# Score maxima taken over 32 tokens of four heads instead of 128 tokens of one, and a later place for the router's second choice, places and scatters

## The chip, the cores and the metric

The kernel runs on one core of one Trainium2 chip. The metric is the device time of one execution in microseconds; the median of several executions is compared. Before the change it is 818.26 us (three runs, 817.12 to 818.61).

## The reference

A transformer layer with attention and a mixture of experts, on x of 8 batches, 256 tokens and 256 features, in 32-bit floats. Cut to what matters here:

```python
q = rope(norm(x) @ Wq)              # 32 query heads of 8
k = rope(norm(x) @ Wk)              # 8 key heads of 8, each for 4 query heads
scores = einsum('bkgtd,bksd->bkgts', q, k) / sqrt(8)
scores = where(causal, scores, -inf)
attn = softmax(scores, axis=-1)
x = x + norm(einsum('bkgts,bksd->bkgtd', attn, v) @ Wo + b_out)

scores = sigmoid(norm(x) @ w_router.T)         # 8 routed experts
topk_w, topk_i = top_k(scores, 2)              # weights divided by their sum
out = sum over the two chosen experts of weight * ((silu(x@wg) * (x@wu)) @ wd)
out = out + two shared experts of the same form
x = x + norm(out)
```

A softmax subtracts each row's maximum before the exponential. A row here is one token of one query head, and its maximum runs over the keys up to that token.

## The kernel before

Tokens lie 128 to a tile, two tiles (tt or t = 0, 1) to a batch. The work up to the router is written as steps put on a timeline by the function `at(when, step, ...)`; the unit of `when` is one batch, and the steps are emitted in the order of `when`. Every engine then executes its own instructions in that order, so the timeline is an order and not a clock. After it come the routed experts, in blocks of 256 rows gathered by expert, and the final norm.

A batch goes through these steps. `project` (L342) multiplies by the weights and VectorE does the rotation of queries and keys (L362, L366, reading PSUM). `split` rounds queries and keys to a high and a low part on POOL. `keysT` and `queriesT` (L404, L436) transpose them on TensorE; the results go to `kst`, which holds the keys, and to `qA`, which holds the queries. In both, three key heads share the 128 partitions, in blocks of 32 rows (J = 3, and NS = 3 such groups c). In `kst` each key head has columns of its own and zeros outside its 32 rows, so one stationary tile of queries, 96 rows high, meets up to three key heads in one stream of columns.

Maxima: for a token tile, `maxima` (L461) computes the scores in PSUM. The stationary operand is one query head slot (group c, head g) of 128 tokens (L472); the columns are the keys of up to three key heads, 128 of them for the first token tile and 256 for the second. A second matmul (L479) adds the causal mask to the last 128 columns of each head, with an identity of 128 rows as the stationary operand. VectorE's reduce (L486) takes the maxima out of a PSUM bank of up to 512 columns. The generator `maxima_of` (L450) lists the calls: per batch 32 pairs of matmuls and 26 reduces. `split_shift` and `shiftT` (L494, L501) round the negated maxima to two parts, transpose them, and send them by three DMAs to rows 96 and up of `qA` (L516).

Weights: `weights_of` (L521) multiplies keys by queries with the shift among the rows (L524), ScalarE takes the exponential (L532) and POOL zeroes what the mask forbids (L534). `values` (L545) multiplies by the values with stationary operands of 32 columns, four side by side (L552). `softmaxed` (L564) transposes the result (L572) and divides.

PSUM: scores, weights and experts' products share five banks (`ps_mm`); transposes, projections, router logits and places share two (`ps_tp`), in turn, and the values' sums have one.

Router: `logits` (L661), then on VectorE `first_choice` (L688) and `second_choice` (L697). `places` (L717) has four small matmuls on TensorE that read the choice (L724, L727) and VectorE work that reads their result; `shares` (L710) makes the weights, and `scatter` (L743) multiplies on POOL and writes records to memory by indirect DMAs on POOL's queue. For all batches but the last, in units of a batch after a base a = b + 1.24, these stand at 0.27, 0.302, 0.37, 0.375 and 0.39. The second token tile's projection of batch b + 3 stands at a + 0.31.

The shared experts (`shared_gate_up`, `shared_down`, L780 and L793) are spread over the attention of later batches from b + 1.5 on.

Of the kernel before, what the change touches and what calls it, by code (L numbers as in the profile page):

```python
# [24 lines left out]
SHIFT = 96  # L25
# [5 lines left out]
def attn_moe_kernel(  # L31
# [47 lines left out]
    nc = tc.nc  # L79
    B, T, D = x.shape  # L80
# [11 lines left out]
    G = 4  # L92
    NKV = NH // G
    NK = NKV * HD
    NC = NKV // G
    J = 3
    NS = -(-NKV // J)
    KR = SHIFT + 2 * J
    QSCALE = HD**-0.5
    FT = 4  # L100
    NTOK = NT * P
# [45 lines left out]
    for b in range(1, B):  # L147
# [6 lines left out]
    nc.scalar.dma_start(out=wr_sb, in_=wr)  # L154


    mask = aconst.tile([P, P], BF16, name="mask")
    nc.gpsimd.memset(mask, 0.0)
    nc.gpsimd.affine_select(
        out=mask,  # L160
        in_=mask,
        pattern=[[-1, P]],
        compare_op=ALU.is_ge,
        fill=NEG,
        base=0,
        channel_multiplier=1,
    )
    ident_b = aconst.tile([P, P], BF16, name="ident_b")
    nc.vector.tensor_copy(ident_b, ident)
    ident_r = aconst.tile([P, P], F32R, name="ident_r")  # L170
    nc.vector.tensor_copy(ident_r, ident)

# [14 lines left out]
    qAs, ksts, v_aug = {}, {}, {}  # L187

    def clear_operands(i):
        qAs[i] = aconst.tile([P, NS * G, T], F32R, name=f"qA_{i}")  # L190
        engine = nc.gpsimd if i > 0 else nc.vector
        engine.memset(qAs[i][:, (NS - 1) * G :, :].bitcast(F32), 0.0)
# [106 lines left out]
    def at(when, step, *args):  # L299
        timeline.append((when, len(timeline), step, args))  # L300
# [100 lines left out]
    def heads_in(c):  # L401
        return min(J, NKV - c * J)
# [33 lines left out]
    def queriesT(b, tt, c):  # L436
        qs = held["qs", b, tt][1]
        n = heads_in(c) * HB
        pt = ps_tp.tile([P, G, P], F32, tag="tp", name=f"pqT{b}_{tt}_{c}")
        for g in range(G):  # L440
            nc.tensor.matmul(
                pt[0:n, g, :],
                lhsT=qs[:, c * G + g, 0:n],
                rhs=ident_r,
                start=True,
                stop=True,
            )
        nc.scalar.copy(qAs[b % 3][0:n, ts(c, G), ts(tt, P)], pt[0:n])

    def maxima_of(b, tt):  # L450

        width = (tt + 1) * P
        for c in range(NS):
            per = min(512 // width, heads_in(c))
            for k0 in range(0, heads_in(c), per):
                nk = min(per, heads_in(c) - k0)
                ng = 512 // (nk * width)
                for g0 in range(0, G, ng):
                    yield c, c * J + k0, nk, g0, ng

    def maxima(b, tt, c, k0, nk, g0, ng):  # L461

        qA, kst = qAs[b % 3], ksts[b % 3]
        if ("nmx", b, tt) not in held:
            held["nmx", b, tt] = small.tile(
                [P, NKV, G], F32, tag="nmx", name=f"nmx{b}_{tt}", bufs=2
            )
        nmx = held["nmx", b, tt]
        width = (tt + 1) * P
        sc = ps_mm.tile([P, ng, nk, width], F32, tag="mm", name="sc")  # L470
        for g in range(ng):
            nc.tensor.matmul(  # L472
                sc[:, g, :, :],
                lhsT=qA[0:SHIFT, c * G + g0 + g, ts(tt, P)],
                rhs=kst[0:SHIFT, k0 : k0 + nk, 0:width],
                start=True,
                stop=False,
            )
            nc.tensor.matmul(  # L479
                sc[:, g, :, width - P :],  # L480
                lhsT=ident_b,
                rhs=mask.unsqueeze(1).to_broadcast([P, nk, P]),
                start=False,
                stop=True,
            )
        nc.vector.tensor_reduce(  # L486
            nmx[:, k0 : k0 + nk, g0 : g0 + ng].rearrange("p k g -> p g k"),
            sc,
            AX.X,
            ALU.max,  # L490
            negate=True,
        )

    def split_shift(b, tt):  # L494
        nmx = held.pop(("nmx", b, tt))
        nhl = small.tile([P, NKV, 2, G], F32R, tag="nhl", name=f"nhl{b}_{tt}", bufs=2)
        nc.vector.tensor_copy(nhl[:, :, 1, :], nmx)
        nc.vector.tensor_tensor(nhl[:, :, 0, :], nmx, nhl[:, :, 1, :], ALU.subtract)
        held["nhl", b, tt] = nhl

    def shiftT(b, tt):  # L501
        nhl = held.pop(("nhl", b, tt))
        pm = ps_tp.tile([2 * NH, P], F32, tag="tp", name=f"pm{b}_{tt}")
        nc.tensor.matmul(
            pm,
            lhsT=nhl.rearrange("p k a g -> p (k a g)"),
            rhs=ident_r,
            start=True,
            stop=True,
        )  # L510
        nm = work.tile([2 * NH, P], F32R, tag="nm", name=f"nm{b}_{tt}")
        nc.vector.tensor_copy(nm, pm)
        for c in range(NS):
            n = 2 * heads_in(c)
            lo = c * J * 2 * G
            nc.sync.dma_start(  # L516
                out=qAs[b % 3][SHIFT : SHIFT + n, ts(c, G), ts(tt, P)].bitcast(F32),
                in_=nm[lo : lo + n * G, :].bitcast(F32),
            )

    def weights_of(b, kv, s, t):  # L521

        sc = ps_mm.tile([P, G, P], F32, tag="mm", name="scT")
        nc.tensor.matmul(  # L524
            sc,
            lhsT=ksts[b % 3][0:KR, kv, ts(s, P)],
            rhs=qAs[b % 3][0:KR, ts(kv // J, G), ts(t, P)],
            start=True,
            stop=True,
        )  # L530
        e = work.tile([P, G, P], F32, tag="ex", name="ex", bufs=EX)
        nc.scalar.activation(e, sc, AF.Exp, scale=QSCALE)  # L532
        if s == t:
            nc.gpsimd.affine_select(  # L534
                out=e,
                in_=e,
                pattern=[[0, G], [1, P]],
                compare_op=ALU.is_ge,
                fill=0.0,
                base=0,  # L540
                channel_multiplier=-1,
            )
        held["ex", b, kv, s, t] = e
# [535 lines left out]
    for b in range(B):  # L1079
# [15 lines left out]
        for tt in range(TT):  # L1095
            for m in maxima_of(b, tt):
                at(when, maxima, b, tt, *m)
                when += 0.032
            at(when + 0.001, split_shift, b, tt)
            at(when + 0.07, shiftT, b, tt)  # L1100
        last = b == B - 1
# [240 lines left out]
```

## Time and profile before

| | |
|---|---|
| median of the runs | 818.26 us |
| the profiled execution's own time | 817.86 us |
| its span, first to last instruction | 815.8 us |
| TensorE clock granted, mean | 0.970 |
| maxima's score matmuls, first and last start | 20.8 and 436.9 us |
| first routed expert's matmul | 548.6 us |

The profile follows one execution. PE is TensorE's matmuls, PEld its loads of stationary operands, DVE is VectorE, ACT ScalarE, POOL GpSimd and SP the engine that issues most DMAs. Busy time is a sum over an engine's instructions. Matmuls are pipelined: one is shown from its start to a modelled end, so that neighbours overlap and their durations add up to more than the time that they take.

In the slices each digit is the busy share of a fortieth of the span, in tenths. A group's row gives line, engine and operation; what is written and what is read; shapes as partitions by elements; the count; busy microseconds and the mean in nanoseconds; and, after the bar, the engine's idle time before these instructions with what ended most of it. A timeline's row gives the start in microseconds from the span's start, the time to the end of the last of the merged instructions, and their count. For matmuls the first shape is rows by columns of the stationary operand, the second the moving operand.

### The profile page before, as it was taken

The page shows a single profiled execution, that of the slowest core. Times are in us where ns is not written, and L with a number is a line of the kernel's source. Part 1 is how long each engine was busy: PE and PEld are TensorE (multiplying, and loading weights), DVE is VectorE, ACT ScalarE, POOL GpSimd, SP SyncE. Part 2 cuts the span into 40 slices and gives each one's busy share as a digit, 9 for nine tenths or more (in the row PEclk, how much of TensorE's full clock was granted, in tenths as well). Part 3 has the DMA queues.
Part 4 walks back from the last instruction along what each step waited for, and adds up shares of the span by engine and source line. Part 5 has one row for each costly group of instructions (what it writes and reads, how often), then busy time and mean ns, then how long its engine had stood idle before and what let it go on. Part 6 is the DMA issues. An engine that isn't in the chain of part 4 may idle for free. (4 is left out here: it accounts for less than half of the span.)

```text
span 815.8 us, 11856 instructions
## 1 busy us (share of the span) xinstructions
PE 761.7 (93%) x3977; PEld 579.3 (71%) x3977; DVE 492.2 (60%) x1412; ACT 251.3 (31%) x552; POOL 344.0 (42%) x620
## 2 busy tenths in 40 slices
PE   5989899999999999999999998799999999999992
PEld 3544467767776776776766657688888888888991
DVE  5756577667668568568666635547655555742226
ACT  2455344334334334333333431121111111111214
POOL 4567456426436436436324441416223434343323
PEclk8799899999999999999999998899999999999997
DMA  5033300000000000000000002365465665758544
GB/s 155 3 88 90 89 16 16 8 22 15 7 23 14 2 29 14 3 29 14 2 29 2 14 14 90 139 226 169 129 206 168 192 218 157 233 149 271 170 81 155
DMA packets 31011, 70.42 MB, mean 86 GB/s; under 512 B 8560, under 2 KB 25456, under 8 KB 28256
## 3 DMA queue, kind: packets, MB, share of 16 engines
q1 hardware_dynamic: 19504, 54.23, 19.2%
q0 software_dynamic: 8128, 9.77, 6.4%
q10 hardware_dynamic: 3312, 5.60, 2.4%
q8 instruction: 34, 0.56, 0.3%
q14 instruction: 33, 0.27, 0.1%
HBM read 55.16 MB, written 11.80 MB: 82 GB/s over the span
## 5 line engine op out<-in xcount | busy, mean ns | idle before, releaser
L780 PE MATMUL gu<-xgT,w 128*128 128x256 f32 (+1 forms) x840 | 163.9, 354 | 1.0 <-ACT xgT L978 0.7
L780 PEld LDWEIGHTS gu<-xgT,w 128*128 128x128 f32 x840 | 144.5, 190 | 18.1 <-ACT xgT L978 1.0
L532 ACT ACTIVATE ex<-scT 128x512 f32<-128x512 f32 x192 | 113.6, 597 | 137.4 <-PE scT L524 124.9
L780 PE MATMUL gu<-x2T,ws_sb 128*128 128x256 f32 x640 | 152.9, 385 | 0.1
L486 DVE TENSOR_REDUCE nmx<-sc 128x2 f32<-128x512 f32 (+2 forms) x208 | 129.3, 643 | 26.4 <-PE sc L479 26.1
L780 PEld LDWEIGHTS gu<-x2T,ws_sb 128*128 128x128 f32 x640 | 119.8, 193 | 21.3 <-ACT ex L532 3.8
L534 POOL TENSOR_SCALAR_AFFINE_SELECT ex<-ex 128x512 f32<-128x512 f32 x128 | 81.0, 639 | 114.3 <-ACT ex L532 114.1
L1014 POOL DMA_INDIRECT sums<-yb,of x37 | 58.5, 1582 | 109.2 <-DVE yb L1013 71.1
L472 PE MATMUL sc<-kst,qA 96*128 96x512 f32 (+2 forms) x256 | 101.3, 426 | 0.8 <-issue 0.5
L524 PE MATMUL scT<-qA,kst 102*128 102x512 f32 x192 | 97.5, 516 | 1.8 <-DMA qA<-nm 1.8
L1003 ACT ACTIVATE sg<-gu 128x256 f32<-128x256 f32 (+1 forms) x105 | 37.6, 358 | 191.1 <-PE gu L780 154.2
L991 DVE STREAM_TRANSPOSE xgT<-xg 32x128 f32<-32x128 f32 x240 | 72.6, 302 | 29.4 <-DMA xg<-rows,of 20.6
L793 PE MATMUL po<-w,act 128*128 128x256 f32 x370 | 83.1, 379 | 0.0
L793 PE MATMUL po<-ws_sb,sact 128*128 128x256 f32 x320 | 74.7, 391 | 4.6 <-DVE sact L816 4.6
L793 PEld LDWEIGHTS po<-w,act 128*128 128x128 f32 x370 | 69.8, 190 | 9.3
L793 PEld LDWEIGHTS po<-ws_sb,sact 128*128 128x128 f32 x320 | 61.6, 196 | 18.3 <-DVE sact L816 5.0
L479 PE MATMUL sc<-mask,ident_b 128*128 128x256 bf16 (+2 forms) x256 | 74.3, 293 | 0.0
L1004 DVE TENSOR_TENSOR act<-sg,gu 128x256 f32<-128x256 f32 (+1 forms) x105 | 38.8, 388 | 56.8 <-ACT sg L1003 56.2
L815 DVE SCALAR_TENSOR_TENSOR th<-th,gu 128x256 f32<-128x256 f32 x70 | 29.4, 419 | 65.8 <-ACT th L814 65.8
L932 POOL DMA_INDIRECT xg<-rows,of x37 | 35.9, 970 | 63.0 <-DMA of<-slots 47.4
L472 PEld LDWEIGHTS sc<-kst,qA 96*128 96x128 f32 x256 | 51.4, 201 | 13.6 <-issue 3.9
L552 PE MATMUL av<-ex,v_aug 128*32 128x512 f32 x384 | 58.3, 605 | 1.3 <-POOL ex L534 1.3
(171 smaller groups left out, 847.8 us busy)
## 6 DMA issues: line engine op xcount, KB each, us to landing
w<-in_routed SPq DMA_DIRECT2D x21, 1920.0 KB
ws_sb<-in_shared ACTq DMA_DIRECT2D x8, 480.0 KB
xs<-in_x SPq DMA_DIRECT2D x8, 256.0 KB
rows<-x2n SPq DMA_DIRECT2D x8, 256.0 KB
acc<-sums SPq DMA_DIRECT2D x4, 512.0 KB
sums<-ya SPq DMA_DIRECT2D x14, 128.0 KB
kst<-kA SPq DMA_DIRECT2D x16, 96.0 KB
out<-acc SPq DMA_DIRECT2D x6, 256.0 KB
```

Of the source, the lines that this page charges most:

```text
L472: nc.tensor.matmul(sc[:, g, :, :], lhsT=qA[0:SHIFT, c * G + g0 + g, ts(tt, P)], rhs=kst[0:SHIFT, k0 : k0 + nk, 0:width], start=True, stop= ...
L479: nc.tensor.matmul(sc[:, g, :, width - P :], lhsT=ident_b, rhs=mask.unsqueeze(1).to_broadcast([P, nk, P]), start=False, stop=True,)
L486: nc.vector.tensor_reduce(nmx[:, k0 : k0 + nk, g0 : g0 + ng].rearrange("p k g -> p g k"), sc, AX.X, ALU.max, negate=True,)
L524: nc.tensor.matmul(sc, lhsT=ksts[b % 3][0:KR, kv, ts(s, P)], rhs=qAs[b % 3][0:KR, ts(kv // J, G), ts(t, P)], start=True, stop=True,)
L532: nc.scalar.activation(e, sc, AF.Exp, scale=QSCALE)
L534: nc.gpsimd.affine_select(out=e, in_=e, pattern=[[0, G], [1, P]], compare_op=ALU.is_ge, fill=0.0, base=0, channel_multiplier=-1,)
L552: nc.tensor.matmul(av[32 * j : 32 * j + 32, :], lhsT=v_aug[b % 3 * TT + s][:, c * G + j, :], rhs=e.rearrange("p g t -> p (g t)"), start=(s ...
L780: nc.tensor.matmul(gu[:, half, :], lhsT=m[:, k, ts(i, P)], rhs=xT[:, k, :], start=(k == 0), stop=(k == KC - 1),)
L793: nc.tensor.matmul(po, lhsT=act[:, k, ts(t, P)], rhs=d[:, k, :], start=(k == 0), stop=(k == ic - 1),)
L991: nc.vector.transpose(to[ts(j, SQ), :, :, ts(i, SQ)], of[ts(i, SQ), :, :, ts(j, SQ)])
L1004: nc.vector.tensor_tensor(act[:, i, :], sg, gu[:, 1, :], ALU.mult)
L1014: put = nc.gpsimd.indirect_dma_start(out=sums, out_offset=bass.IndirectOffsetOnAxis(ap=of[:, t, 1:2], axis=0), in_=y, in_offset=None, comp ...
```

## The change

The tile of `maxima` becomes 32 tokens (QB) of all four query heads that share a key head: 128 stationary columns as before, but four such tiles (TQ) to a token tile. Each needs only the keys up to its own end, so widths run from 32 to 256 in steps of 32. `qA` is laid out to match, with the four heads' 32 tokens next to each other. The mask is 32 by 32, added to the last 32 columns of each head, through a stationary operand `token_of` of 32 rows and 128 columns. A reduce takes as many key heads as fit a bank, which may take matmuls from two groups c. Per batch there are still 32 pairs of matmuls, with 9,216 score columns instead of 12,288, and 21 reduces instead of 26. On ScalarE, `queriesT` writes and the exponential reads in the new order; the exponential's output and all after it are as before.

On the timeline the maxima are 0.04 apart instead of 0.032, and for all batches but the last the second choice moves from 0.302 to 0.345 after the base, places from 0.37 to 0.445, shares from 0.375 to 0.447, and the two scatters from 0.39 and 0.42 to 0.46 and 0.49.

```diff
+    QB = P // G
+    TQ = P // QB
...
-    mask = aconst.tile([P, P], BF16, name="mask")
+    mask = aconst.tile([QB, QB], BF16, name="mask")
...
-    ident_b = aconst.tile([P, P], BF16, name="ident_b")
-    nc.vector.tensor_copy(ident_b, ident)
+    token_of = aconst.tile([QB, P], BF16, name="token_of")
+    nc.vector.tensor_copy(
+        token_of.rearrange("p (g q) -> p g q", g=G),
+        ident[0:QB, 0:QB].unsqueeze(1).to_broadcast([QB, G, QB]),
+    )
...
-        qAs[i] = aconst.tile([P, NS * G, T], F32R, name=f"qA_{i}")
+        qAs[i] = aconst.tile([P, NS, T // QB, G * QB], F32R, name=f"qA_{i}")
...
-        nc.scalar.copy(qAs[b % 3][0:n, ts(c, G), ts(tt, P)], pt[0:n])
+        to = qAs[b % 3][0:n, c, ts(tt, TQ), :].rearrange("p i (g q) -> p g i q", g=G)
+        nc.scalar.copy(to, pt[0:n].rearrange("p g (i q) -> p g i q", i=TQ))
...
     def maxima_of(b, tt):
 
-        width = (tt + 1) * P
-        for c in range(NS):
-            per = min(512 // width, heads_in(c))
-            for k0 in range(0, heads_in(c), per):
-                nk = min(per, heads_in(c) - k0)
-                ng = 512 // (nk * width)
-                for g0 in range(0, G, ng):
-                    yield c, c * J + k0, nk, g0, ng
+        for i in range(TQ):
+            width = (tt * TQ + i + 1) * QB
+            steps = -(-NKV // (512 // width))
+            per = -(-NKV // steps)
+            for k0 in range(0, NKV, per):
+                yield i, k0, min(per, NKV - k0)
...
-        sc = ps_mm.tile([P, ng, nk, width], F32, tag="mm", name="sc")
-        for g in range(ng):
+        width = (tt * TQ + i + 1) * QB
+        sc = ps_mm.tile([P, nk, width], F32, tag="mm", name="sc")
+        for c in range(k0 // J, -(-(k0 + nk) // J)):
+            k, z = max(k0, c * J), min(k0 + nk, c * J + J)
+            part = sc[:, k - k0 : z - k0, :]
             nc.tensor.matmul(
-                sc[:, g, :, :],
-                lhsT=qA[0:SHIFT, c * G + g0 + g, ts(tt, P)],
-                rhs=kst[0:SHIFT, k0 : k0 + nk, 0:width],
+                part,
+                lhsT=qA[0:SHIFT, c, tt * TQ + i, :],
+                rhs=kst[0:SHIFT, k:z, 0:width],
                 start=True,
                 stop=False,
             )
             nc.tensor.matmul(
-                sc[:, g, :, width - P :],
-                lhsT=ident_b,
-                rhs=mask.unsqueeze(1).to_broadcast([P, nk, P]),
+                part[:, :, width - QB :],
+                lhsT=token_of,
+                rhs=mask.unsqueeze(1).to_broadcast([QB, z - k, QB]),
                 start=False,
                 stop=True,
             )
...
+        nc.vector.tensor_reduce(nmx[:, k0 : k0 + nk, i], sc, AX.X, ALU.max, negate=True)
...
-            rhs=qAs[b % 3][0:KR, ts(kv // J, G), ts(t, P)],
+            rhs=qAs[b % 3][0:KR, kv // J, ts(t, TQ), :],
...
-        nc.scalar.activation(e, sc, AF.Exp, scale=QSCALE)
+        nc.scalar.activation(
+            e.rearrange("p g (i q) -> p g i q", i=TQ),
+            sc.rearrange("p i (g q) -> p g i q", g=G),
+            AF.Exp,
+            scale=QSCALE,
+        )
...
-                when += 0.032
+                when += 0.04
...
-        at(a + 0.302, second_choice, b)
-        at(a + 0.37, places, b)
-        at(a + 0.375, shares, b)
+        at(a + 0.345, second_choice, b)
+        at(a + 0.445, places, b)
+        at(a + 0.447, shares, b)
         for t in range(TT):
-            at(a + 0.39 + 0.03 * t, scatter, b, t)
+            at(a + 0.46 + 0.03 * t, scatter, b, t)
```

More of the change, by code (lines that the diff above doesn't have):

```diff
@@ L161, in attn_moe_kernel @@
         in_=mask,
-        pattern=[[-1, P]],
+        pattern=[[-1, QB]],
         compare_op=ALU.is_ge,
@@ L189, in clear_operands @@
     def clear_operands(i):
-        qAs[i] = aconst.tile([P, NS * G, T], F32R, name=f"qA_{i}")
+        qAs[i] = aconst.tile([P, NS, T // QB, G * QB], F32R, name=f"qA_{i}")
         engine = nc.gpsimd if i > 0 else nc.vector
-        engine.memset(qAs[i][:, (NS - 1) * G :, :].bitcast(F32), 0.0)
+        engine.memset(qAs[i][:, NS - 1, :, :].bitcast(F32), 0.0)
         t = ksts[i] = aconst.tile([P, NKV, T], F32R, name=f"kst_{i}")
@@ L447, in queriesT, with maxima @@
             )
-        nc.scalar.copy(qAs[b % 3][0:n, ts(c, G), ts(tt, P)], pt[0:n])
+        to = qAs[b % 3][0:n, c, ts(tt, TQ), :].rearrange("p i (g q) -> p g i q", g=G)
+        nc.scalar.copy(to, pt[0:n].rearrange("p g (i q) -> p g i q", i=TQ))
     def maxima_of(b, tt):
-        width = (tt + 1) * P
-        for c in range(NS):
-            per = min(512 // width, heads_in(c))
-            for k0 in range(0, heads_in(c), per):
-                nk = min(per, heads_in(c) - k0)
-                ng = 512 // (nk * width)
-                for g0 in range(0, G, ng):
-                    yield c, c * J + k0, nk, g0, ng
-    def maxima(b, tt, c, k0, nk, g0, ng):
+        for i in range(TQ):
[4 more added lines that the diff above has]
+                yield i, k0, min(per, NKV - k0)
+    def maxima(b, tt, i, k0, nk):
         qA, kst = qAs[b % 3], ksts[b % 3]
@@ L465, in maxima @@
             held["nmx", b, tt] = small.tile(
-                [P, NKV, G], F32, tag="nmx", name=f"nmx{b}_{tt}", bufs=2
+                [P, NKV, TQ], F32, tag="nmx", name=f"nmx{b}_{tt}", bufs=2
             )
         nmx = held["nmx", b, tt]
-        width = (tt + 1) * P
-        sc = ps_mm.tile([P, ng, nk, width], F32, tag="mm", name="sc")
-        for g in range(ng):
+        width = (tt * TQ + i + 1) * QB
[3 more added lines that the diff above has]
+            part = sc[:, k - k0 : z - k0, :]
             nc.tensor.matmul(
-                sc[:, g, :, :],
-                lhsT=qA[0:SHIFT, c * G + g0 + g, ts(tt, P)],
-                rhs=kst[0:SHIFT, k0 : k0 + nk, 0:width],
+                part,
+                lhsT=qA[0:SHIFT, c, tt * TQ + i, :],
+                rhs=kst[0:SHIFT, k:z, 0:width],
                 start=True,
@@ L485, in maxima @@
             )
[L486 to L492, printed above, removed]
+        nc.vector.tensor_reduce(nmx[:, k0 : k0 + nk, i], sc, AX.X, ALU.max, negate=True)
     def split_shift(b, tt):
         nmx = held.pop(("nmx", b, tt))
-        nhl = small.tile([P, NKV, 2, G], F32R, tag="nhl", name=f"nhl{b}_{tt}", bufs=2)
+        nhl = small.tile([P, NKV, 2, TQ], F32R, tag="nhl", name=f"nhl{b}_{tt}", bufs=2)
         nc.vector.tensor_copy(nhl[:, :, 1, :], nmx)
@@ L514, in shiftT @@
             n = 2 * heads_in(c)
-            lo = c * J * 2 * G
+            lo = c * J * 2 * TQ
             nc.sync.dma_start(
-                out=qAs[b % 3][SHIFT : SHIFT + n, ts(c, G), ts(tt, P)].bitcast(F32),
-                in_=nm[lo : lo + n * G, :].bitcast(F32),
+                out=qAs[b % 3][SHIFT : SHIFT + n, c, ts(tt, TQ), :].bitcast(F32),
+                in_=nm[lo : lo + n * TQ, :].bitcast(F32),
             )
     def weights_of(b, kv, s, t):
-        sc = ps_mm.tile([P, G, P], F32, tag="mm", name="scT")
+        sc = ps_mm.tile([P, TQ, G * QB], F32, tag="mm", name="scT")
         nc.tensor.matmul(
```

## The prediction

> **What bounds the kernel now.** I read the page's busy times and slices first, then the busy times in stretches of 20 us, then the groups by shape, and last the order of TensorE's instructions inside one batch.
>
> ```profile
> PE 761.7 (93%) x3977; PEld 579.3 (71%) x3977; DVE 492.2 (60%) x1412; ACT 251.3 (31%) x552; POOL 344.0 (42%) x620
> ...
> PE   5989899999999999999999998799999999999992
> ```
> ```profile
> L486 DVE TENSOR_REDUCE nmx<-sc 128x2 f32<-128x512 f32 (+2 forms) x208 | 129.3, 643 | 26.4 <-PE sc L479 26.1
> ...
> L472 PE MATMUL sc<-kst,qA 96*128 96x512 f32 (+2 forms) x256 | 101.3, 426 | 0.8 <-issue 0.5
> ...
> L479 PE MATMUL sc<-mask,ident_b 128*128 128x256 bf16 (+2 forms) x256 | 74.3, 293 | 0.0
> ```
>
> TensorE is the bound: 93% over all, and 18.9 to 20.0 us of every 20 between 140 and 400 us. The first score matmul of the weights (L524) of batches 2, 3, 4, 5 and 6 starts at 141.4, 203.4, 265.7, 327.9 and 389.9 us: a batch takes 62.2 us of TensorE's time, and what leaves its queue there leaves the span. The reduces (129 us of VectorE) idle 26 us waiting for TensorE, so they are the follower, except in the start-up stage. The maxima run from 20.8 to 437 us; nothing after that is touched, it only starts earlier.
>
> The two rows L472 and L479 say 176 us, but matmuls overlap and their ends are modelled; what a pair (score, then mask) costs is read from start to start, in the timeline of TensorE:
>
> ```profile
> 187.04 0.36 PE L472 MATMUL sc<-kst,qA 96*128 96x256 f32 x1
> 187.24 0.23 PE L479 MATMUL sc<-mask,ident_b 128*128 128x128 bf16 x1
> 187.28 0.36 PE L472 MATMUL sc<-kst,qA 96*128 96x256 f32 x1
> 187.49 0.23 PE L479 MATMUL sc<-mask,ident_b 128*128 128x128 bf16 x1
> 187.53 0.36 PE L472 MATMUL sc<-kst,qA 96*128 96x256 f32 x1
> ```
>
> 256+128 columns take 0.245 us. Elsewhere 256+256 columns take 0.25 (162.54 to 162.79 us) and 512+256 take 0.36 (184.55 to 184.91). So 256 mask columns cost no more than 128: the mask stream hides the load of the next stationary operand. A load is seen bare in the router's logits (eight-column matmuls, eight in 0.92 us: 0.115 each) and, in bf16, in the place matmuls (0.03 to 0.05 each). My price of a pair: its score columns at 2.4 per ns, plus 0.14 us (a bare load of each kind), more only where the mask stream is over 0.11 us. That gives 0.246 for both small forms, 0.352 for 512+256, 0.348 for 384+384.
>
> **The pairs.** Before, a batch has 8 pairs of 384+384, 4 of 256+256, 12 of 512+256, 8 of 256+128: 2.78 + 0.98 + 4.22 + 1.97 = 9.96 us. After, there are again 32 pairs, with 9,216 score columns in place of 12,288 and at most 96 mask columns each: 32 x 0.14 + 9,216/2,400 = 4.45 + 3.84 = 8.29 us. **The saving is 1.67 us a batch, 13.4 us in eight.** By columns alone (9,216 score and mask columns fewer) it would be 3.84 us a batch; the loads do not shrink, and they eat more than half of it.
>
> **The mode of the array.** The mask's stationary operand shrinks from 128 rows to 32, so the built program gives that matmul a tile of 32 rows by 128 columns, between matmuls on the whole array: two changes of mode in each of 256 pairs. The trace has no tile of fewer rows, but two of fewer columns:
>
> ```profile
> 168.63 0.28 PE L479 MATMUL sc<-mask,ident_b 128*128 128x256 bf16 x1
> 168.84 1.06 PE L552 MATMUL av<-ex,v_aug 128*32 128x512 f32 x8
> 169.84 0.56 PE L441 MATMUL pqT<-ident_r,qs 128*96 128x128 f32 x4
> ```
> ```profile
> 200.76 0.50 PE L524 MATMUL scT<-qA,kst 102*128 102x512 f32 x1
> 201.10 0.40 PE L441 MATMUL pqT<-ident_r,qs 128*64 128x128 f32 x4
> 201.34 0.22 PE L504 MATMUL pm<-ident_r,nhl 128*64 128x128 f32 x1
> 201.40 1.94 PE L780 MATMUL gu<-x2T,ws_sb 128*128 128x256 f32 x8
> ```
>
> Into the 32-column tiles the mask takes 0.21 us to the next start where it takes 0.12 into the shared expert (184.79 to 184.91): 0.09 more. In the single starts of the trace the two groups of four stand 0.434 apart and the next work starts 0.522 after the second: 0.09 again on the way out. Into the 64-column tile the start comes after 0.34 us, as it does into whole-array work after L524 (0.31 to 0.32), and out of it after 0.06, the price of one such matmul: nothing. The Trainium skill (TensorEngine Tiling (Array Packing), Tiling Modes, Key Properties) says that a change of tiling mode, not merely of tile, drains the engine. By the 32-column row and that rule a pair would pay 0.18 us, 256 pairs 47 us, and the change loses; by the 64-column row it pays nothing. The 64-column matmuls are nearer in form: one tile, at the array's corner, between whole-array matmuls, with no second tile beside it, whereas the 32-column work runs four tiles at once. I take 0, and keep 0 and 0.18 us for the range.
>
> **The router.** Four times the weighted values' transpose waits for the rotation:
>
> ```profile
> L572 PE MATMUL pav<-ident,avs 128*128 128x128 f32 x128 | 19.9, 279 | 4.3 <-DVE rb L366 4.0 <-DVE avs L561 0.3
> ```
>
> There are two buffers for these PSUM tiles. One holds the projection until VectorE's rotation (L362, L366) has read it, the other holds the places, and VectorE does the second choice (eight instructions of 0.16 to 0.18 us and their gaps, 181.25 to 182.8 us) before the rotation. In the new order the rotation stands before the second choice, and places come after the next transpose, which so takes the buffer before the projection's and finds it free. **4.0 us go.** What is late next: the second choice is 0.1 of a batch (6 us) ahead of the places that wait for it, and queued behind its 1.6 us on VectorE are the softmax division of that transpose (read again only by a later transpose) and a maximum, with five PSUM buffers in front of TensorE. The four scatters of a batch (0.2 us and an indirect DMA of 1.03 us each on POOL) move 4.4 us later, past POOL's splits and masks of weights; POOL is busy 7 to 12 us of each 20, and their records are first read 0.7 of a batch after the last of those moved. The last batch's router keeps its times. Cost 0.
>
> **VectorE.** The three forms lie on a line, 0.55 us at 384 elements and 0.68 at 512: 0.15 + 1.04 ns an element. 168 reduces of 73,728 elements in all in place of 208 of 98,304: 25.2 + 76.7 = 102 us, against 133 by the same line: 31 us less. Beside TensorE that is worth nothing. In the start-up, to about 50 us, reduces run back to back (five in 2.4 us from 28.25 us, seven in 4.3 from 38.96), and TensorE is not full: bounds 0 and 8 us (two batches at 3.9). POOL's setup and its masks of weights end the waits soon after, so I take 2.
>
> **The rest, at nothing.** The mask constants change size during the start-up's wait for x. The maxima end 0.008 of a batch later at the latest (pace 0.04 for 21 steps, 0.84, was 0.032 for 26, 0.83), 14 us ahead of the first weights that need that half's shift, and its three transfers take 2.4 us; the first half's shift is 5 us earlier. The transfers stay three of the same bytes, in longer runs. ScalarE's exponential now reads PSUM in runs of 32; nearest is VectorE's rotation, which reads runs of four (160 elements in 0.315 us, between 128 in 0.292 and 256 in 0.420): no charge. Were it half as dear again, ScalarE at 5 to 10 us of each 20 would still follow.
>
> **Sum:** -13.4 - 4.0 - 2 = -19.4 us. Against the profiled execution's own 817.9 us (span 815.8, 2.1 around it) that is 798.5; against the median of 818.3 us, **799 us**.
>
> **Rivals.**
> - *The mode change drains (0.29).* 0.18 us a pair is 47 us: 818.3 + 47 - 19.4 = 846 us; draining on one side only, 0.09, gives 822. The place is between score and mask and between mask and the next load, and it decides from 0.076 us a pair (19.4/256). For it: the 32-column row and the rule. Against: the 64-column row.
> - *The small pairs have a floor (0.14).* 256+128 and 256+256 both take 0.25 us; if that is a floor for any pair, the 18 pairs of a batch with up to 256 score columns cost 4.5 us, and the other 14 (5,984 columns) by my price 1.96 + 2.49: 8.95 us in place of 9.96. 8 + 4 + 2 us are saved: 804 us. Against: the bare loads, 0.115 and 0.03, leave 0.10 of such a floor unexplained, and my price gives the same 0.25 without it.
> - *The wait moves (in the forecast's own range).* If second choice or scatters make a new wait of a microsecond a batch, the 4 us come back: 803 us.
>
> **Numbers.** Forecast 0.55, its own range 790 to 805; drain 0.29; floor 0.14; 0.02 for others. The range 786 to 838 reaches from the column count's side down to two thirds of the drain's price. No change is what lies within 0.2% (1.6 us), about what a measurement of this kernel can tell. Faster 0.67 (forecast and floor, less what the moved wait and a half-sized drain take from them), slower 0.28 (the drain above 0.08 us a pair), same 0.05.
>
> **What would show it.** In the changed kernel's timeline a pair of 192+32 columns from start to start: 0.22 us if my price holds, 0.25 if there is a floor, 0.35 to 0.40 if the mode drains. The batch period: near 59.5 us, or 60 with the floor, or 65 with the drain. The row of the transpose should lose its wait for the rotation. The reduces should come to about 102 us in 168. I am wrong if the pairs take more than before while their columns shrink.

## The result and the profile after

The changed kernel is slower: a median of 858.9 us (four runs, 854.5 to 867.5) beside 817.7 us of the kernel before in the same comparison (four runs), a ratio of 1.0485 (95% interval 1.0411 to 1.0560). The forecast was 799 us, and the range ended at 838.

The profile is of an execution of 854.5 us with a span of 852.8 us and a mean granted clock of 0.943 (before: 0.970). Its page:

```profile
PE 803.9 (94%) x3977; PEld 600.1 (70%) x3977; DVE 468.7 (55%) x1372; ACT 251.1 (29%) x552; POOL 345.4 (41%) x620
...
PE   4999899999999999999999989879999999999992
...
PEclk9568877999999999999999999889999999999997
...
L493 DVE TENSOR_REDUCE nmx<-sc 128x2 f32<-128x384 f32 (+5 forms) x168 | 102.2, 611 | 58.2 <-PE sc L486 57.8
```

and three rows of its groups by line, with the row of the mask's load before the change below them:

```profile
L486 PE MATMUL sc<-mask,token_of 32*128 32x64 bf16 (+2 forms) x256 | 51.9, 203 | 0.0
...
L486 PEld LDWEIGHTS <-token_of 32*128 32x128 bf16 x256 | 23.5, 92 | 54.6 <-issue 45.9
...
L578 PE MATMUL pav<-ident,avs 128*128 128x128 f32 x128 | 20.7, 285 | 0.3 <-DVE avs L567 0.3
```
```profile
L479 PEld LDWEIGHTS <-ident_b 128*128 128x128 bf16 x256 | 25.5, 99 | 41.4 <-issue 35.2
```

Three things were meant to shrink and did: the reduces (129.3 to 102.2 us), the mask stream (74.3 to 51.9 us) and the transpose's wait for the rotation (4.0 us, gone). VectorE idles 58 us for the scores where it idled 26: it follows TensorE more than before. TensorE's busy time rose by 42 us although it executes the same 3,977 matmuls over fewer columns. The rows do not say why. Before the mask's load 45.9 us of idle are put down to "issue", a wait for nothing that the profile shows, but there were 35.2 before the change too; and the mean duration of a mask matmul fell from 293 to 203 ns.

The starts show it. This is the timeline of TensorE in the steady state (start, time to the modelled end, instruction), then that of its loads in the same stretch:

```profile
168.59 0.35 PE L479 MATMUL sc<-kst,qA 96*128 96x192 f32 x1
168.87 0.21 PE L486 MATMUL sc<-mask,token_of 32*128 32x96 bf16 x1
169.02 0.33 PE L479 MATMUL sc<-kst,qA 96*128 96x128 f32 x1
```
```profile
168.59 0.19 PEld L479 LDWEIGHTS sc<-kst,qA 96*128 96x128 f32 x1
168.87 0.09 PEld L486 LDWEIGHTS <-token_of 32*128 32x128 bf16 x1
169.01 0.19 PEld L479 LDWEIGHTS sc<-kst,qA 96*128 96x128 f32 x1
```

192 score columns and 96 mask columns take 0.43 us from start to start; the prediction's price for them was 0.22. The mask starts 0.28 us after its score matmul, and the next score matmul 0.15 us after the mask. The load for that score matmul starts only 0.14 us after the mask matmul, and each matmul follows its own load at once.

The second thing is the clock. Busy time by stretches (from:to, length, busy us and count of PE, PEld, DVE, ACT and POOL, granted clock, DMA share, GB/s), first after, then before:

```profile
20.00:40.00 20.00, 19.71 (x73) 12.46 (x72) 9.69 (x21) 8.28 (x16) 9.17 (x23) 0.59 0.01 3
40.00:60.00 20.00, 20.00 (x67) 10.75 (x67) 8.36 (x21) 7.60 (x15) 10.20 (x25) 0.52 0.18 43
...
100.00:120.00 20.00, 18.73 (x72) 11.38 (x71) 9.28 (x25) 6.40 (x12) 7.38 (x16) 0.66 0.22 60
```
```profile
20.00:40.00 20.00, 18.91 (x90) 11.64 (x88) 13.86 (x30) 10.16 (x20) 9.96 (x23) 0.77 0.02 5
40.00:60.00 20.00, 16.15 (x83) 9.32 (x82) 10.66 (x26) 11.51 (x23) 13.29 (x30) 0.91 0.32 87
...
100.00:120.00 20.00, 18.80 (x118) 12.04 (x117) 13.82 (x43) 9.37 (x19) 11.14 (x27) 1.00 0.05 16
```

In the start-up TensorE runs at about half its clock for long stretches, and gets 67 matmuls done from 40 to 60 us where it did 83.

Three marks divide the span: the first weights matmul of batch 2 (start-up), the mean distance of that matmul between batches 2 and 6 (the period), and the rest. Half-clock time is twice the clock missing in all stretches before 250 us: read in short stretches the granted clock is 0.50 or 1.00 (changed kernel: 0.50 from 45 to 50 us, 1.00 from 61 to 65 us).

| | start of batch 2's weights | period | half-clock time | span |
|---|---|---|---|---|
| before | 141.4 us | 62.1 | 23.9 | 815.8 |
| after | 163.7 us | 65.2 | 71.7 | 852.8 |

Of the 37 us, 22.3 are in the start-up, 12.4 in four periods and 2 in the rest.

Executions over 1.5% above the fastest of their kernel (one each of the changed kernel, e10 and e11, the profiled one of e13, three of e6's four) count as slow and are left out of the ratios but not of the medians; for e6 the remaining one is given and no ratio, and of e13's profile only the batches at full clock, from 178.9 us on, are read.

### The profile page after: what moved, and what is told of

Read it like the earlier page. It is cut to its first block, busy times and chain, and to the rows that moved or that the text cites. A ratio compares the mean times of both kernels' runs of the same rounds, so it can differ in the third digit from the quotient of the medians.

```text
span 852.8 us, 11813 instructions
## 1 busy us (share of the span) xinstructions
PE 803.9 (94%) x3977; PEld 600.1 (70%) x3977; DVE 468.7 (55%) x1372; ACT 251.1 (29%) x552; POOL 345.4 (41%) x620
## 4 chain that ended last, share of the span: by engine, by line
PE 85%; DVE 7%; POOL 4%; issue 2%; ACT 1%; DMA 1%; ACTq 0%; POOLq 0%; DVEq 0%
PE gu L786 35%; PE po L799 18%; PE sc L479 6%; PE scT L525 6%; PE av L558 5%; PE sc L486 3%; PE pq L352 3%; PE pqT L446 2%; PE py L605 2%; PE pav L578 2%; PE pl L671 1%; POOL r L290 1%; DVE st L284 1%; DVE nmx L493 1%; POOL ex L540 1%
## 5 line engine op out<-in xcount | busy, mean ns | idle before, releaser
L786 PE MATMUL gu<-x2T,ws_sb 128*128 128x256 f32 x640 | 156.2, 391 | 0.0
L493 DVE TENSOR_REDUCE nmx<-sc 128x2 f32<-128x384 f32 (+5 forms) x168 | 102.2, 611 | 58.2 <-PE sc L486 57.8
L525 PE MATMUL scT<-qA,kst 102*128 102x512 f32 x192 | 101.5, 536 | 1.7 <-DMA qA<-nm 1.7
L479 PE MATMUL sc<-kst,qA 96*128 96x192 f32 (+11 forms) x256 | 102.5, 400 | 0.3 <-issue 0.2
L799 PEld LDWEIGHTS po<-ws_sb,sact 128*128 128x128 f32 x320 | 61.5, 195 | 18.4 <-DVE sact L822 5.0
L479 PEld LDWEIGHTS sc<-kst,qA 96*128 96x128 f32 x256 | 53.4, 209 | 21.7 <-issue 8.1
L486 PEld LDWEIGHTS <-token_of 32*128 32x128 bf16 x256 | 23.5, 92 | 54.6 <-issue 45.9
L820 ACT ACTIVATE th<-gu 128x256 f32<-128x256 f32 x70 | 26.9, 384 | 110.3 <-PE gu L786 107.3
```

The source lines that it names most:

```text
L479: nc.tensor.matmul(part, lhsT=qA[0:SHIFT, c, tt * TQ + i, :], rhs=kst[0:SHIFT, k:z, 0:width], start=True, stop=False,)
L486: nc.tensor.matmul(part[:, :, width - QB :], lhsT=token_of, rhs=mask.unsqueeze(1).to_broadcast([QB, z - k, QB]), start=False, stop=True,)
L493: nc.vector.tensor_reduce(nmx[:, k0 : k0 + nk, i], sc, AX.X, ALU.max, negate=True)
L525: nc.tensor.matmul(sc, lhsT=ksts[b % 3][0:KR, kv, ts(s, P)], rhs=qAs[b % 3][0:KR, kv // J, ts(t, TQ), :], start=True, stop=True,)
L786: nc.tensor.matmul(gu[:, half, :], lhsT=m[:, k, ts(i, P)], rhs=xT[:, k, :], start=(k == 0), stop=(k == KC - 1),)
L799: nc.tensor.matmul(po, lhsT=act[:, k, ts(t, P)], rhs=d[:, k, :], start=(k == 0), stop=(k == ic - 1),)
```

## The experiments

The kernel before ran at 817.7 to 819.0 us in all comparisons. The table holds every run; ratios are against it, with 95% intervals. Start-up, period and half-clock time are of the profiled execution.

| run | median us | ratio | start-up | period | half clock |
|---|---|---|---|---|---|
| e1_rows128 | 818.0 | 0.9990 (0.9965–1.0015) | 150.2 | 61.5 | 51.0 |
| e2_no_mask | 812.0 | 0.9930 (0.9887–0.9973) | 141.1 | 61.3 | 44.3 |
| e3_router_only | 814.7 | 0.9951 (0.9930–0.9972) | 139.4 | 61.4 | 17.0 |
| e4_maxima_only | 871.7 | 1.0640 (1.0593–1.0686) | 168.3 | 67.7 | 81.8 |
| e5_rows128_shift | 816.8 | 1.0001 (0.9950–1.0051) | 144.0 | 60.7 | 37.5 |
| e6_rows64 | 846.3 (one; the others 867) | – | 155.4 | 65.3 | 51.2 |
| e7_rows128_shift_warm | 814.1 | 0.9961 (0.9914–1.0008) | 142.0 | 60.7 | 17.1 |
| e8_no_mask_shift | 808.4 | 0.9909 (0.9858–0.9961) | 138.1 | 60.1 | 34.0 |
| e9_rows128_tp3 | 814.1 | 0.9954 (0.9918–0.9991) | 140.3 | 60.0 | 30.7 |
| e10_router_tp3 | 818.4 | 1.0015 (0.9975–1.0055) | 137.3 | 61.3 | 13.6 |
| e11_no_mask_tp3 | 801.7 | 0.9784 (0.9703–0.9865) | 137.3 | 58.7 | 30.6 |
| e12_rows128_tp3_warm | 809.8 | 0.9897 (0.9833–0.9961) | 140.7 | 60.0 | 20.5 |
| e13_before_extra32 | 877.0 | 1.0647 (1.0549–1.0745) | – | 69.0 | – |
| e14_before_extra128 | 826.5 | 1.0086 (1.0055–1.0117) | 142.4 | 63.7 | 17.1 |
| e15_rows128_tp3_shift_warm | 809.2 | 0.9873 (0.9819–0.9926) | 141.8 | 58.8 | 20.4 |
| e16_no_mask_tp3_shift_warm | 796.6 | 0.9734 (0.9656–0.9811) | 140.1 | 56.8 | 20.4 |

The time that the leading theory of an expectation gave was met by e3, e7, e12, e14 and e16. It was missed by 1 to 4 us in e4, e11, e13, e15 and e6, by more in e1, e2, e5, e8 and e9, and e10 came out as its rival had it; the text says what each shows.

### Is it the height of the mask's stationary tile?

**e1_rows128** pads the mask and its stationary operand from 32 to 128 rows, with zeros in the operand; columns, counts and order are those of the changed kernel.

```diff
-    mask = aconst.tile([QB, QB], BF16, name="mask")
-    token_of = aconst.tile([QB, P], BF16, name="token_of")
+    mask = aconst.tile([128, QB], BF16, name="mask")
+    token_of = aconst.tile([128, P], BF16, name="token_of")
+    nc.vector.memset(token_of, 0.0)
...
-                rhs=mask.unsqueeze(1).to_broadcast([QB, z - k, QB]),
+                rhs=mask.unsqueeze(1).to_broadcast([128, z - k, QB]),
```

> The changed kernel with its mask and token_of padded with zero rows to 128, so that no matmul is a tile of 32 rows; columns, order and schedule stay. Theory D (each pair pays two mode changes, and the drained array also loses its clock in the start-up): a pair from start to start falls back to about 0.14 us plus its columns, the half-clock time before 150 us falls from 72 to about 24 us, total 795 to 805 us. Rival C (fewer columns keep TensorE less busy in the start-up, so that it loses its clock whatever the mode): the pairs get cheaper, but the half-clock time stays near 70 us, total 830 to 840. Rival S (the schedule makes the waits): stays near 859.

818.0 us: four times the rows, and 41 us less than the changed kernel. The timeline of e1 at the same pair:

```profile
217.55 0.34 PE L480 MATMUL sc<-kst,qA 96*128 96x192 f32 x1
217.73 0.22 PE L487 MATMUL sc<-mask,token_of 128*128 128x96 bf16 x1
217.77 0.31 PE L480 MATMUL sc<-kst,qA 96*128 96x128 f32 x1
```
```profile
217.73 0.10 PEld L487 LDWEIGHTS <-token_of 128*128 128x128 bf16 x1
217.73 0.20 PEld L480 LDWEIGHTS sc<-kst,qA 96*128 96x128 f32 x1
```

0.22 us instead of 0.43, which is the price in the prediction. The mask follows after 0.18 us (was 0.28) and the next score matmul after 0.04 (was 0.15). Over all steady pairs, from start to start in both traces, score plus mask take 13.68 us a batch in the changed kernel and 8.63 in e1: 5.05/32 = 0.158 us a pair, 0.097 on the way into the 32-row tile and 0.060 on the way out. 256 times 0.158 is 40 us; the medians differ by 41. That the two agree so well is partly chance: of the 5.05 us a batch, the period shows 3.8, while the start-up is 13.5 us shorter. The duration column shows none of it (203 ns a mask before the padding, 214 with it).

The loads show what the price is. In e1 the load for the next score matmul starts with the mask matmul and goes on beneath it. In the changed kernel the next load starts 0.113, 0.126 and 0.140 us after the start of a mask of 32, 64 and 96 columns (medians of 116 starts from 180 to 420 us, all within 0.001 us; e1: 0.002 at each width): the time of the mask's columns, at the prediction's 2.4 per ns, and another 0.10 us. No load begins beneath a mask any more, which is what a drain looks like.

**e6_rows64** pads to 64 rows instead.

```diff
+    mask = aconst.tile([64, QB], BF16, name="mask")
+    token_of = aconst.tile([64, P], BF16, name="token_of")
...
+                rhs=mask.unsqueeze(1).to_broadcast([64, z - k, QB]),
```

> The changed kernel with mask and token_of padded to 64 rows, so that the mask matmul is a tile of 64 rows. Theory D (any change of row mode drains): like the changed kernel, 850 to 865 us, pairs within 0.02 us of its own. Rival (as with the 64-column tile, only the 32-row mode is dear): like the padded run, 815 to 822.

Its period, 65.3 us, and its 13.72 us of score and mask a batch are those of 32 rows: half the array costs what a quarter does. A pair in its timeline, 0.42 us for 192+64 columns from start to start:

```profile
166.32 0.36 PE L480 MATMUL sc<-kst,qA 96*128 96x192 f32 x1
166.61 0.20 PE L487 MATMUL sc<-mask,token_of 64*128 64x64 bf16 x1
166.74 0.70 PE L787 MATMUL gu<-x2T,ws_sb 128*128 128x256 f32 x2
```

In all these pairs the score's stationary operand has 96 rows and stands beside operands of 128, in e1 without any such price: it is not every difference in height that is dear.

**e13_before_extra32** and **e14_before_extra128** take the pair out of the question: in the kernel before, each mask matmul is followed by one more matmul of 32 columns that adds zero, with a stationary operand of 32 rows (e13) or of 128 (e14), written n here.

```diff
+    zero_b = aconst.tile([n, P], BF16, name="zero_b")
+    nc.vector.memset(zero_b, 0.0)
...
-                stop=True,
+                stop=False,
+            )
+            nc.tensor.matmul(
+                sc[:, g, 0, 0:32],
+                lhsT=zero_b,
+                rhs=mask[0:n, 0:32],
+                start=False,
+                stop=True,
             )
```

> The kernel before with one more matmul in each of its 256 pairs: 32 bf16 columns times a stationary operand of 32 rows of zeros, which adds zero. Theory D (the change of row mode is dear by itself): 0.12 to 0.16 us a pair more than the same with 128 rows, and more half clock in the start-up: 845 to 875 us. Rival (dear only with the new tiles and their columns): within 5 us of the same with 128 rows.

> The kernel before with one more matmul in each of its 256 pairs: 32 bf16 columns times a stationary operand of 128 rows of zeros, which adds zero. Both theories: a bare bf16 load and 32 columns, 0.03 to 0.06 us a pair, partly into waits: 820 to 832 us.

The medians differ by 50.5 us, 0.20 a pair, with nothing between them but rows. Part of that is the clock: e13's fastest execution, at e14's mean granted clock (0.974), takes 864.3 us, 38 us more than e14, 0.15 a pair. The timeline of e13, then of e14, at the same pair:

```profile
218.36 0.38 PE L474 MATMUL sc<-kst,qA 96*128 96x256 f32 x1
218.59 0.23 PE L481 MATMUL sc<-mask,ident_b 128*128 128x128 bf16 x1
218.75 0.18 PE L488 MATMUL sc<-mask,zero_b 32*128 32x32 bf16 x1
218.86 0.50 PE L533 MATMUL scT<-qA,kst 102*128 102x512 f32 x1
```
```profile
178.62 0.36 PE L474 MATMUL sc<-kst,qA 96*128 96x256 f32 x1
178.82 0.23 PE L481 MATMUL sc<-mask,ident_b 128*128 128x128 bf16 x1
178.89 0.18 PE L488 MATMUL sc<-mask,zero_b 128*128 128x32 bf16 x1
178.91 0.49 PE L533 MATMUL scT<-qA,kst 102*128 102x512 f32 x1
```

Into the 32-row tile 0.16 us instead of 0.07, out of it 0.11 instead of 0.02: 0.18 more, in a kernel without any other part of the change. The sums of a steady batch give 0.17 a pair (mask 6.94 against 3.87 us, extra matmul 3.67 against 1.37). The price belongs to the change of height, not to the change's short streams.

### The two halves of the change

**e3_router_only** is the kernel before with the new router times; **e4_maxima_only** is the changed kernel with the old ones (the same lines the other way round).

```diff
-        at(a + 0.302, second_choice, b)
-        at(a + 0.37, places, b)
-        at(a + 0.375, shares, b)
+        at(a + 0.345, second_choice, b)
+        at(a + 0.445, places, b)
+        at(a + 0.447, shares, b)
         for t in range(TT):
-            at(a + 0.39 + 0.03 * t, scatter, b, t)
+            at(a + 0.46 + 0.03 * t, scatter, b, t)
```

> The kernel before with the changed times of second choice, places, shares and scatters alone. Theory D: the transpose's four waits of 1.0 us for the rotation go and nothing else changes: 813 to 815 us. Rival S: slower than before, 825 to 840.

> The changed kernel with the router's old times: the maxima's change alone. Theory D: as slow as the changed kernel or some 4 us slower, 855 to 868. Rival S: back towards 800 to 825.

The router alone gains 4.1 us, as it was priced. The maxima alone cost 53 us, so with them the router is worth some 13 us by the two ratios, three times as much. The traces place it only in part: e4 waits 4.0 us for the rotation, as the kernel before does, but its period is 2.5 us longer than the changed kernel's. Why was not tried.

**e2_no_mask** drops the mask matmul from the changed kernel (the score matmul ends the sum itself).

> The changed kernel without any mask matmul: the maxima then run over the keys up to the end of the 32-token tile, up to 31 of them after the token, so they may be larger than the row's own maximum; the causal mask of the weights stays. Theory D: no mode change and 256 matmuls and loads fewer, a pair's 0.14 us plus columns becomes the larger of columns and a load of 0.11 us, about 4.6 us a batch in place of 8.3: 765 to 785 us, and little half clock. Rival C: even less TensorE work in the start-up, so at least as much half clock as the changed kernel has, 72 us or more, and no less than 810 us. Rival S: near 840.

812.0 us: with no mask at all, and so no change of height, the kernel gains 6 us over e1 and still only 7 over the kernel before. The forecast had 13 us for the pairs with their masks. That, and e1's 818 where the same sum said 799, is the second question.

### Where the gain of the pairs went

The periods of e1, e2 and e3 are 61.5, 61.3 and 61.4 us: those of the new maxima and of the old, with the same router times, are one. Between the starts of e1's trace, score and mask take 3.2 us a batch less than in e3's (8.63 against 11.87). But the first start after a weights matmul comes later, 1.3 us a batch in all, after the shared experts' down projections 0.5, after their gate 0.4, after the shift's transpose (pm) 0.4 and after the transpose of the router's input (px) 0.35: 3.0 us given back. The profile shows about half of that as idle time of TensorE; in the other half the next start comes later without any. The waits of TensorE in e1 from 140 to 480 us (waiting for whom: us, times, longest):

```profile
PE pm L506 <- DVE kA L431: 4.3, 4, 1.3
PE pav L579 <- DVE avs L568: 2.8, 4, 1.8
PE pqT L447 <- DVE kA L431: 1.4, 3, 0.5
```

Before, the same view began with the transposes' 4.0 us for the rotation and held no pm. `pm` has one of the two transpose buffers, and the buffer it needs is emptied by VectorE's copy of the transposed keys (kA). In the timeline of e1, the bracket giving the idle time before:

```profile
171.21 0.48 PE L526 MATMUL scT<-qA,kst 102*128 102x512 f32 x1
172.94 0.24 PE L506 MATMUL pm<-ident_r,nhl 128*64 128x128 f32 x1 [1.25 <-DVE kA L431]
```

**e5_rows128_shift** moves the first token tile's `shiftT` on e1, later and past that copy; **e8_no_mask_shift** does it on e2.

```diff
-            at(when + 0.07, shiftT, b, tt)
+            at(b - 0.59 if tt == 0 else when + 0.07, shiftT, b, tt)
```

> The run with the mask padded to 128 rows, and besides the first half's shift transpose put back to where it stands in the kernel before (0.39 after the maxima's start instead of 0.33). Theory W (in the padded run that transpose waits some 1.3 us a batch for a PSUM buffer behind VectorE, and pushes 0.7 us of further waits on): the batch period falls from 61.5 to near 59.5 us, total 804 to 810 us. Rival B (something else holds a batch at 61.4 us, since the kernel with the router's move alone, the padded one and the one without masks all show it): the period stays at 61.4 and the total at 816 to 819.

> The run without mask matmuls (maxima over keys up to the end of the 32-token tile), with the first half's shift put back. Theory W: the period falls from 61.3 to near 58.5 us, total 794 to 804 us. Rival B: the period stays at 61.3 and the total at 810 to 813.

In e5 the wait changed its name, in the same view:

```profile
PE pqT L447 <- DVE kA L431: 4.0, 5, 1.2
PE pav L579 <- DVE avs L568: 2.4, 2, 1.8
PE pqT L447 <- POOL qs L405: 1.3, 1, 1.3
```

Whoever asks next for a buffer waits for VectorE. The periods fall by 0.8 us (e5) and 1.2 (e8), less than half of what the theory of the wait had. 816.8 us is no gain that can be told from e1; in e8 the same move is worth some 4 us by the medians, inside the intervals.

**e9_rows128_tp3**, **e10_router_tp3** and **e11_no_mask_tp3** give the transposes a third buffer, taken from the scores, on e1, e3 and e2.

```diff
-    ps_mm = ctx.enter_context(tc.tile_pool(name="ps_mm", bufs=5, space=PSUM))
-    ps_tp = ctx.enter_context(tc.tile_pool(name="ps_tp", bufs=2, space=PSUM))
+    ps_mm = ctx.enter_context(tc.tile_pool(name="ps_mm", bufs=4, space=PSUM))
+    ps_tp = ctx.enter_context(tc.tile_pool(name="ps_tp", bufs=3, space=PSUM))
```

> The run with the mask padded to 128 rows, with three PSUM buffers for transposes and projections instead of two and four for scores and products instead of five. Theory W (what the cheaper pairs free goes into waits for those two buffers, which VectorE empties late): the waits of 1.3 us a batch of the transposes for VectorE go, the period falls from 61.5 to 58.5 to 59.5 us, total 800 to 810. Rival P (four banks for the scores are too few, or the work of the batch is bound elsewhere): the period stays at 61 or above, total 815 or more.

> The kernel before with the router's new times and the same three and four buffers. Theory W: it has 1.5 us a batch of such waits, so its period falls by 1 us at most, from 61.4 to 60.4 or more, total 808 to 815; the run above is then ahead of it by 2 us a batch or so. Rival P: slower than with two and five, 816 or more.

> The run without mask matmuls (maxima over keys up to the end of the 32-token tile), with three and four buffers. Theory W: it has most to regain, the period falls from 61.3 to 57 to 58.5 us, total 785 to 800. Rival P: 61 us and 810.

With the new maxima the period falls by 1.5 us (e9) and 2.6 (e11), and the medians by 4 and 10 us; with the old maxima by 0.1, and the median rises by 4, as the rival had it. So two buffers were enough for the old maxima, and became a limit with the smaller pairs. The rise has a place of its own, the routed experts (below).

### The clock of the start-up

**e7_rows128_shift_warm** fills TensorE in the first three batches on e5: ahead of each tile of scores, a matmul over as many columns whose result is overwritten. **e12_rows128_tp3_warm** does so on e9.

```diff
+        if b < 3:
+            nc.tensor.matmul(
+                sc.rearrange("p k w -> p (k w)").rearrange("p (a q) -> p a q", q=QB),
+                lhsT=token_of,
+                rhs=mask.unsqueeze(1).to_broadcast([P, nk * width // QB, QB]),
+                start=True,
+                stop=True,
+            )
```

> The padded run with the shift put back, and in the maxima of batches 0 to 2 one idle bf16 matmul over each bank ahead of the real ones, whose product is overwritten: 21 a batch of up to 0.24 us each at full clock, 12 us of work in all. Theory C (in the start-up TensorE loses its clock because it has too little to stream): half-clock time before 250 us falls from 51 to 30 us or less, and the total is below that of the same kernel without the idle matmuls, or equal. Rival (the clock falls because TensorE waits on others, and more work only adds): half-clock time stays, total 6 to 12 us above it.

> The first run of this call with the idle matmuls over each bank of the maxima of batches 0 to 2, whose product is overwritten. Theory C: half-clock time before 250 us near 17 us instead of 35 to 51, total 0 to 6 us below the run without them. Rival: 6 to 12 us above it.

The stretches of e5, then of e7:

```profile
20.00:40.00 20.00, 19.78 (x83) 14.52 (x82) 10.41 (x22) 8.99 (x17) 9.30 (x23) 0.51 0.02 6
40.00:60.00 20.00, 15.56 (x90) 8.78 (x88) 10.19 (x26) 11.40 (x21) 14.16 (x31) 0.91 0.24 66
```
```profile
20.00:40.00 20.00, 19.13 (x108) 13.28 (x107) 10.94 (x26) 9.75 (x20) 9.36 (x23) 0.75 0.04 9
40.00:60.00 20.00, 16.15 (x96) 9.03 (x96) 9.75 (x25) 11.93 (x23) 14.17 (x31) 1.00 0.30 83
```

More work, and more of it done in the same 20 us. Half-clock time falls from 37.5 to 17.1 us, that of the kernel before or less, and the four executions of e7 have mean granted clocks of 0.968 to 0.974, where e5's have 0.951 to 0.961. In the medians it is worth 2.7 us from e5 to e7 and 4.3 from e9 to e12, and the intervals against the kernel before separate neither pair; start-up marks move by 2 us (e5 to e7) and not at all (e9 to e12).

### All together

**e15_rows128_tp3_shift_warm** puts the padded mask, the third buffer, the later shift and the warm start together; **e16_no_mask_tp3_shift_warm** has no mask in place of the padded one.

> Mask padded to 128 rows, three buffers for transposes and four for scores, the first half's shift transpose at 0.39, and the idle matmuls in batches 0 to 2. Theory W: the wait of 0.67 us a batch of that transpose for the split goes too, period 59.0 to 59.6 us, total 803 to 808. Rival: the wait moves on, 809 to 812.

> The same without mask matmuls: maxima over keys up to the end of the 32-token tile. Theory W: period 57.5 to 58.3 us, total 793 to 800. Rival: 800 to 804.

e15 keeps the causal mask and takes 809.2 us, 1.3% below the kernel before (e12, without the moved shift, takes 809.8); e16 takes 796.6 us, 2.7% below. Part of e15's gain is lost again. Its period is 1.2 us below e12's, and yet the medians agree. From the first routed expert's matmul to the end, the traces have 274.2 us before (541.6 to 815.8; the 548.6 in the table ahead of the prediction is not that matmul's start) and 274.6 in e1, but 276.4 in e12 and 279.2 in e15. TensorE waits there for VectorE's products, in e15 (535 us to the end) and in e10 (536 us to the end):

```profile
PE gu L795 <- DVE act L1019: 1.9, 4, 0.5
PE gu L795 <- DVE yb L1028: 1.5, 2, 1.1
```
```profile
PE gu L780 <- DVE act L1004: 2.5, 4, 0.7
```

where before it waited for VectorE not at all. This is the price of the third buffer. The experts' products (`gu`, and the one that `yb` is made from) stand in the same PSUM buffers as the scores, and these went from five to four. All six kernels with four have 276.4 to 279.7 us here; e10 differs from e3 (274.3 us) in the buffers alone and has 279.1, which also accounts for its slower median. Of the profiled kernels with five, all have 274.2 to 275.2 but e4 and e8 (279.9 and 282.2), each with one wait of 3.9 us for `yb` that was not looked into.

## Why the prediction was wrong

**The step that failed is "The mode of the array": "I take 0".** It measured 0.158 us a pair over the steady batches and 0.15 to 0.18 in isolation (e13 against e14), 41 us between the medians with and without it (e1), and so carried the result past the point that the text itself gave for it, 0.076 us a pair. The pair that the text named as the sign, 192+32 columns, takes 0.35 us in the changed kernel, the drain's value. The prediction had two rows and a rule. It chose the 64-column row as nearer in form (one tile, at the corner, between whole-array matmuls). The 32-column row, put aside because four tiles run at once, was the nearer in price: 0.09 in and 0.09 out, where the 32-row tile has 0.10 and 0.06. A tile of fewer columns and one of fewer rows are not the same form, and nothing in the trace had fewer rows; so the choice should have gone by the two sources that spoke against the change, the dear row and the Trainium skill (TensorEngine Tiling (Array Packing), Tiling Modes, Key Properties). Here the rule agrees with the trace: the next load waits for the mask's columns and 0.10 us more. This case's 64-column matmuls don't pay it. Why they don't is open: the profile shows that 64 columns were used, not that the array was set to a tile of that width, and no experiment varied columns.

**The rival of the drain** came out in kind, and 13 us below the result. Its period (65) is the measured one (65.2), in part by luck: score and mask were to rise by 4.1 us a batch and rose by 2.0 (11.64 to 13.68), while the rest of a batch rose by 1.0. Its time, 846 us, had the price of a pair a little too high (47 us for 40) and kept all the gains of the forecast, which did not come.

**"What leaves its queue there leaves the span" failed too**, and it is worth 19 us: e1, the change without the drain, takes 818 where the same sum gave 799. The pairs themselves shrank by more than was predicted: the new ones take 8.63 us a batch between starts in e1 (8.29 predicted), the old ones 11.64 before (9.96 by the same price, which was 1.7 us short). But TensorE at 19 to 20 us of every 20 was not free to move up: a full engine whose buffers are just emptied in time gains only until the next buffer. Waits for the two transpose buffers took much of it back: a third buffer returns 1.5 us of the period in e9 and 2.6 in e11, against 0.1 in e10. With the shift moved too, the period is 58.8 us, even below the 59.5 that was predicted. In time, e12 wins back 8 of the 19 us and e15 hardly more. Of the 10 that are left in e15, 5 stand in the routed experts, the third buffer's price; and the start-up, in which the smaller pairs and reduces were to gain, ends where it did before (141.8 us, with the idle matmuls in it, and 141.4).

**The start-up** was priced at 2 us of gain for VectorE's faster reduces. The reduces are as predicted (102.2 us in 168), but TensorE's clock was not in the sum. The profiled executions were at half clock for 24 us before, 51 in e1 and 72 in the changed kernel. One execution is not enough to split this between the shorter streams and the drain, for e6, which has the drain, shows 51 as well. The mean granted clocks of all executions keep the order: 0.969 to 0.980 before, 0.951 to 0.965 in e1, 0.926 to 0.945 in the changed kernel. Of the 22 us that the start-up lost, the profiles of e1 and the changed kernel put 13.5 on the drain, its own price and its clock together (e1's profiled execution stood 5 us above its median, the changed kernel's 4 below). e7 and e12 show that the clock comes back with idle matmuls, but that this alone is worth 3 to 4 us by the medians, with overlapping intervals.

**The router** was right: the wait of 4.0 us went, e3 gained 4.1, and scatters and second choice made no new wait of a microsecond a batch. **The floor** is refuted: in e1's timeline the next start comes 0.22 us after 192+96 columns, below 0.25, and 0.17 us after 192+32. **The rest at nothing** held where it can be read: ScalarE's exponential takes 597 ns a piece in the new order, as in the old.

What stays open: why 64 columns are not dear where 64 rows are, how the start-up's clock is split between shorter streams and drain, and why the router's move is worth more in the drained kernel.

## What to carry to other kernels

A smaller operand is not a cheaper one: where a matmul stands between others that use the whole array, fill its stationary operand up to 128 rows with zeros rather than leave it at 32 or 64, and price a tile shape that the trace doesn't hold by its dearest relative. Read matmuls from start to start: the cost of a change of shape stands in no duration, but in when the next load starts. And when the bounding engine gets less to do, ask who empties the buffers that it will reach earlier, and whether it stays busy enough to keep its clock; a buffer that is moved to one stage is missing in another that shares it.

## What the hardware showed unasked

- A stationary operand of 32 or of 64 rows between whole-array matmuls costs 0.15 to 0.18 us more than one of 128 rows, and the two heights cost the same (periods 65.2 and 65.3 us). In the changed kernel the next load starts 0.10 us after the mask's columns are through, instead of with the mask.
- In the changed kernel, TensorE was granted 0.52 of its clock from 40 to 60 us while the profile has it busy for all of the 20 us: busy by the profile isn't busy for the clock. The Trainium skill (TensorE: Matmul & The Clock Gate, Part 1: The HAM clock gate) names two states of the clock, half and full, set by how busy the array has been; the 0.50 and 1.00 of short stretches, and the fall of half-clock time in e7 with matmuls that compute nothing, agree. That a drain counts as idle there would fit, and was not tested by itself.
- A mask stream of 32 to 96 columns at full height costs about 0.05 us a pair (e9 against e11: 12.4 us in 256).
